# Keys and values in fixed lines: the order of a loop over eight groups of rows is written out, the value copy moves to VectorE, and a square root is written to PSUM

## The chip, the cores and the metric

The kernel runs on one core of a Trainium2 chip. The metric is device time in microseconds (us) of one execution; the time quoted for a kernel is the median of several executions.

## The reference, cut to what matters

The network has four parts on a residual stream x of 8 x 512 = 4096 rows of 128 floats, all in fp32: a local convolution, a small feed-forward network whose operands are quantised to four bits, a linear-attention part that trains a small network on its own keys and values, and a mixture of experts. Only the start of the third part is touched by this change:

```python
x = layernorm(x)
qkv = x @ qkv_w + qkv_b
q, k, v = jnp.split(qkv, 3, axis=-1)                    # 128 columns each
k = k.reshape(B, S, 16, 8)                              # 16 heads of 8
k = k / (jnp.linalg.norm(k, axis=-1, keepdims=True) + 1e-6) * kn_scale + kn_bias
...
for _ in range(2):                                      # training steps
    grads = jax.grad(loss_fn)(theta)                    # of mean((swish(k @ gate) * (k @ val)) @ proj - v)^2
    theta = muon_update(theta, grads)
```

The keys k and the values v of all 4096 rows must be there before the first training step has gone through them; the queries are made later, in pieces, between the steps.

## The kernel before, in words

The 4096 rows lie in SBUF as 32 tiles of 128 rows. They are worked on in `NG` = 8 groups of `G` = 4 tiles (512 rows). The stream x stays in SBUF for the whole kernel.

The kernel is written in a framework that takes the instructions of all engines in program order, works out the waits between them, and lets its own scheduler choose the order on each engine from due times it estimates. Where the author wants a fixed order he passes the instructions of an engine through a `Line` (line 105 of the kernel): each instruction of a line is put behind the one before it.

The touched stage is the first block of `ttt` (lines 824 to 863). For each group g it does this, in the order of its lines:

- `normal(g)`, lines 839 to 849. The layer norm's statistics come from VectorE, for four groups at once (`norm.stats`, `norm.newton`). ScalarE then applies them (`norm.apply`, line 583: four instructions of 128x128, tile `xn`), TensorE transposes `xn` (line 848, four matmuls against the identity), and ScalarE copies the transposed rows out of PSUM into `xt` (line 849).
- `rows_of`, line 799. TensorE multiplies the transposed rows by the key and value columns of the weight (four matmuls 128x256; the profile shows each as two records). The PSUM tile `rows` holds 4 x 256 numbers for each partition, two banks, and there are two such tiles.
- Line 856. ScalarE copies the value half into `v`.
- `heads`, lines 802 to 814. ScalarE squares the key half (line 805, tile `sq`); VectorE sums the squares of each head (line 807, 128x512 to 128x64, tile `nrm`); ScalarE takes the root in place (line 808); VectorE adds 1e-6 (line 809), inverts (line 810) and multiplies the keys by it (line 811, tile `k`).
- `turned`, lines 816 to 821. TensorE transposes the normed keys (line 820), and ScalarE takes them out of PSUM with the scale and shift of the heads (line 821, tile `kt`).
- Line 861. GpSimd applies the same scale and shift to the untransposed keys in place, two instructions. It may start only when the transposes of these keys have been read.

After the loop, line 863 adds a bias to each group of x on GpSimd; the scheduler spreads these eight instructions over the stage. The scheduler has put the normed rows `xn` of groups 0 to 3 ahead of the first `rows` matmul. From there its order on TensorE is: rows 0, rows 1, key transposes 0, `xn` transposes 2, rows 2, key transposes 1, `xn` transposes 3, rows 3, and so on: rows run one group ahead of the key transposes, and the transposes that rows are made from stand directly in front of them.

In front of the stage stands the last group of the feed-forward network (`fp4_ffn`, lines 627 to 730), whose quantisation goes back and forth: GpSimd scales (line 619, tile `v`), ScalarE takes magnitudes into PSUM (line 621), VectorE rounds (lines 622 and 623), GpSimd scales back (line 624, tile `hq`), TensorE transposes (line 708), ScalarE copies (line 711), TensorE multiplies (lines 714 and 716) and ScalarE writes x (line 720). Behind the stage stands `gradients` (lines 1073 to 1144), where for each tile TensorE has two forward products (lines 1087 and 1089), and GpSimd four instructions that make the derivative `ds` (lines 1100 to 1103).

Of the kernel before, what the change touches and what calls it, by code (L numbers as in the profile page):

```python
# [7 lines left out]
F32 = mybir.dt.float32  # L8
I32 = mybir.dt.int32
U32 = mybir.dt.uint32  # L10
AF = mybir.ActivationFunctionType
# [106 lines left out]
def grp(t, g):  # L118
    return t[:, g * G : (g + 1) * G, :]
# [434 lines left out]
class Norm:  # L554
# [1 line left out]


    def __init__(self, cx, pool, name, plus=0.0):
        self.cx, self.pool, self.name, self.plus = cx, pool, name, plus
        self.mv = pool.tile([P, NT, 2], F32, tag=f"{name}mv", name="mv")  # L560
        self.rs = pool.tile([P, NT], F32, tag=f"{name}rs", name="rs")
        self.off = pool.tile([P, NT], F32, tag=f"{name}off", name="off")
# [17 lines left out]
    def apply(self, g, dst):  # L580
        for j in range(G):
            i = g * G + j
            self.cx.nc.scalar.activation(
                dst[:, j, :], self.cx.x[:, i, :], AF.Identity, bias=self.off[:, i : i + 1], scale=self.rs[:, i : i + 1]
            )


UP = 1024
# [184 lines left out]
def ttt(cx):  # L773
# [10 lines left out]
    with ExitStack() as st:  # L784
# [6 lines left out]
        v = kv.tile([P, NT, D], F32, tag="v", name="v")  # L791
        kt = kv.tile([P, T], F32, tag="kt", name="kt")

        def rows_of(ps, tag, g, lo, hi):

            out = ps.tile([P, G, hi - lo], F32, tag=tag, name="rows")
            for j in range(G):
                at = slice(g * W + j * P, g * W + (j + 1) * P)
                nc.tensor.matmul(out[:, j, :], xt[:, at], w_qkv[:, lo:hi], start=True, stop=True)  # L799
            return out  # L800

        def heads(pool, src, dst):

            sq = pool.tile([P, G, D], F32, tag="sq", name="sq")
            nc.scalar.activation(sq, src, AF.Square)
            nrm = pool.tile([P, G, H], F32, tag="nrm", name="nrm")
            nc.vector.tensor_reduce(nrm, sq.rearrange("p j (h d) -> p j h d", d=DH), AX.X, ALU.add)
            nc.scalar.activation(nrm, nrm, AF.Sqrt)
            nc.vector.tensor_scalar(nrm, nrm, 1e-6, None, ALU.add)
            nc.vector.reciprocal(nrm, nrm)  # L810
            nc.vector.tensor_tensor(
                dst.rearrange("p j (h d) -> p j h d", d=DH), src.rearrange("p j (h d) -> p j h d", d=DH),
                nrm.unsqueeze(3).to_broadcast([P, G, H, DH]), ALU.mult,
            )

        def turned(ps, tag, src, i, dst):

            tp = ps.tile([P, W], F32, tag=tag, name="tp")
            for j in range(G):
                nc.tensor.transpose(tp[:, j * P : (j + 1) * P], src[:, j, :], cx.ident)  # L820
            nc.scalar.activation(dst, tp, AF.Identity, bias=cols[:, i, 1:2], scale=cols[:, i, 0:1])


        with ExitStack() as s1:
            wp = s1.enter_context(tc.tile_pool(name="c1_w", bufs=1))
            p2 = s1.enter_context(tc.tile_pool(name="c1_p2", bufs=2))
            ps = s1.enter_context(tc.tile_pool(name="c1_ps", bufs=4, space=PSUM))
            ps_q = s1.enter_context(tc.tile_pool(name="c1_psq", bufs=2, space=PSUM))
            norm = Norm(cx, wp, "ln", plus=1.0)
            total = ps.tile([P, 3 * D], F32, tag="t", name="total")  # L830
# [5 lines left out]
                nc.tensor.transpose(pp[:, c * P : (c + 1) * P], proj[:, c, :], cx.ident)  # L836
            nc.scalar.copy(proj_t, pp)

            def normal(g):
                if g % 4 == 0:  # L840
                    for i in range(g, g + 4):
                        norm.stats(i)
                    norm.newton(g, g + 4)
                xn = p2.tile([P, G, D], F32, tag="xn", name="xn")
                norm.apply(g, xn)
                tp = ps.tile([P, W], F32, tag="t", name="tp")
                for j in range(G):
                    nc.tensor.transpose(tp[:, j * P : (j + 1) * P], xn[:, j, :], cx.ident)
                nc.scalar.copy(xt[:, g * W : (g + 1) * W], tp)

            normal(0)
            for g in range(NG):
                if g + 1 < NG:
                    normal(g + 1)
                kvr = rows_of(ps_q, "kv", g, D, 3 * D)
                nc.scalar.copy(grp(v, g), kvr[:, :, D:])
                heads(p2, kvr[:, :, :D], grp(k, g))
                turned(ps, "t", grp(k, g), 1, kt[:, g * W : (g + 1) * W])
                r = grp(k, g).rearrange("p j (h d) -> p j h d", d=DH)
                for c, op in ((scale, ALU.mult), (shift, ALU.add)):  # L860
                    nc.gpsimd.tensor_tensor(r, r, c.unsqueeze(1).unsqueeze(1).to_broadcast([P, G, H, DH]), op)
            for g in range(NG):
                nc.gpsimd.tensor_tensor(grp(cx.x, g), grp(cx.x, g), b_o.unsqueeze(1).to_broadcast([P, G, D]), ALU.add)

        def queries(step):

            with ExitStack() as s3:
                pool = s3.enter_context(tc.tile_pool(name=f"q_p{step}", bufs=2))
                ps = s3.enter_context(tc.tile_pool(name=f"q_ps{step}", bufs=1, space=PSUM))
                for g in range(step * NG // STEPS, (step + 1) * NG // STEPS):  # L870
                    pq = rows_of(ps, "q", g, 0, D)
                    q = pool.tile([P, G, D], F32, tag="q", name="q")
                    heads(pool, pq, q)
                    yield
                    turned(ps, "q", q, 0, qt[:, g * W : (g + 1) * W])
                    yield


# [640 lines left out]
```

## Time and profile before

| what | value |
|---|---|
| median of three runs | 1273.8 us (1272.79 to 1276.15) |
| the profiled execution's own time | 1273.81 us |
| its span, first to last instruction | 1272.1 us |
| mean granted TensorE clock | 0.957 of full speed |
| busy share of the span: TensorE, VectorE, GpSimd, ScalarE | 86%, 60%, 58%, 39% |
| the touched stage, first `rows` matmul to the last group's key transposes | 400.14 to 441.17 us |

In the profile PE is TensorE, PEld its weight loads, DVE is VectorE, ACT is ScalarE and POOL is GpSimd. Times within an execution count from the start of the span. A row of the timeline has the start, the duration, the engine, the line and the tile written, and in brackets how long the engine was idle before and what released it. The granted clock (PEclk) is the share of full speed at which TensorE was let run.

### The profile page before, as it was taken

How to read it: one execution, taken by the hardware profiler on the slowest of the kernel's cores; microseconds unless marked ns; L12 is line 12 of the kernel's file. 1: busy time of each engine (PE TensorE's matmuls, PEld its weight loads, DVE VectorE, ACT ScalarE, POOL GpSimd, SP SyncE). 2: the span in 40 equal slices, each digit the busy share in tenths (PEclk: the TensorE clock that was granted, in tenths of full speed). 3: DMA queues.
4: the chain of work that ended last, by engine and by line, in shares of the span. 5: the costliest groups of instructions: out<-in, count | busy, mean ns of one | idle time of the engine just before them, and what ended most of it. 6: DMA issues, size and time to landing. Idle time of an engine off the chain costs nothing.

```text
span 1272.1 us, 15373 instructions
## 1 busy us (share of the span) xinstructions
PE 1090.9 (86%) x5219; PEld 650.0 (51%) x5219; DVE 765.5 (60%) x1761; ACT 494.0 (39%) x1009; POOL 743.3 (58%) x724
## 2 busy tenths in 40 slices
PE   5899998537877599999998899999989996599992
PEld 2334343225556445555557455555566664377872
DVE  6899999788885454444446444444455877033254
ACT  4646644346556632222234322222253342234331
POOL 3346755735554688888860688888700456355453
PEclk9899999958999999999999999999999998699997
DMA  5322444970000000000000000000000111212277
GB/s 152 87 79 80 124 110 139 356 208 1 1 1 1 0 1 1 1 1 1 1 1 1 0 1 1 1 1 1 1 1 1 34 39 46 62 51 68 68 183 212
DMA packets 66895, 67.26 MB, mean 53 GB/s; under 512 B 6928, under 2 KB 48735, under 8 KB 66817
## 3 DMA queue, kind: packets, MB, share of 16 engines
q1 hardware_dynamic: 59296, 56.57, 15.1%
q0 software_dynamic: 4608, 8.43, 2.1%
q10 hardware_dynamic: 2912, 1.29, 0.4%
q8 instruction: 41, 0.67, 0.2%
q14 instruction: 38, 0.30, 0.1%
HBM read 40.00 MB, written 27.13 MB: 53 GB/s over the span
## 4 chain that ended last, share of the span: by engine, by line
PE 50%; DVE 12%; ACT 5%; POOL 5%; issue 5%; DMA 2%; POOLq 0%; DVEq 0%; SPq 0%; ACTq 0%
PE ph L1135 5%; PE sum L1110 4%; PE pp L1125 4%; PE sum L1109 4%; PE sum L1111 4%; PE pa L1087 4%; PE ph L1429 4%; PE pb L1089 4%; PE po L1442 4%; PE pt L1118 2%; PE gu L692 2%; POOL v L619 1%; DVE ht L915 1%; PE a L975 1%; PE rows L799 1%
## 5 line engine op out<-in xcount | busy, mean ns | idle before, releaser
L1100 POOL TENSOR_TENSOR ds<-sw,s 128x512 f32<-128x512 f32 x64 | 81.7, 1276 | 86.8 <-DVE sw L1095 86.8
L1102 POOL TENSOR_TENSOR ds<-ds,s 128x512 f32<-128x512 f32 x64 | 111.4, 1740 | 5.0
L1330 POOL DMA_INDIRECT rows<-xr,slot x64 | 62.8, 982 | 73.8 <-DVE rs L93 45.1
L1093 ACT COPY b<-pb 128x512 f32<-128x512 f32 x64 | 37.5, 586 | 161.5 <-PE pb L1089 161.0
L1456 POOL DMA_INDIRECT res<-ye,xe x60 | 58.5, 975 | 66.2 <-DVE ye L1454 28.1
L1097 DVE TENSOR_TENSOR h<-sw,b 128x512 f32<-128x512 f32 x64 | 50.4, 787 | 70.6 <-ACT b L1093 70.3
L1432 ACT ACTIVATE ht<-ph,b 128x512 f32<-128x512 f32 (+2 forms) x100 | 55.9, 589 | 92.7 <-PE ph L1429 91.2
L402 POOL TENSOR_TENSOR pr<-base,en 128x512 f32<-128x512 f32 x48 | 72.7, 1545 | 32.4 <-ACT en L364 32.3
L1101 POOL TENSOR_TENSOR ds<-sw,ds 128x512 f32<-128x512 f32 x64 | 82.8, 1294 | 5.0
L1103 POOL TENSOR_TENSOR ds<-ds,b 128x512 f32<-128x512 f32 x64 | 81.5, 1273 | 5.0
L1125 PEld LDWEIGHTS pp<-proj,ht 128*128 128x128 f32 x512 | 67.1, 191 | 30.7 <-issue 29.4
L411 DVE TENSOR_TENSOR pr<-base,w 128x3072 f32<-128x3072 f32 x24 | 79.7, 3319 | 1.7 <-ACT w L362 1.7
L1120 ACT COPY ht<-pt 128x512 f32<-128x512 f32 x64 | 37.5, 586 | 102.1 <-PE pt L1118 102.1
L1442 PE MATMUL po<-w,ht 128*128 128x128 f32 (+1 forms) x640 | 77.1, 277 | 0.0
L1095 DVE TENSOR_TENSOR sw<-pa,s 128x512 f32<-128x512 f32 x64 | 44.2, 691 | 54.2 <-ACT s L1091 54.2
L1429 PE MATMUL ph<-xt,w 128*128 128x512 f32 (+2 forms) x200 | 72.8, 508 | 3.7 <-DVE xt L1417 3.7
L1442 PEld LDWEIGHTS po<-w,ht 128*128 128x128 f32 (+1 forms) x640 | 73.7, 187 | 0.7
L1137 DVE TENSOR_TENSOR db<-ph,sw 128x512 f32<-128x512 f32 x64 | 44.2, 691 | 47.1 <-PE ph L1135 47.1
L1135 PE MATMUL ph<-proj_t,dpt 128*128 128x512 f32 x128 | 71.6, 641 | 0.0
L420 PE MATMUL cv<-pr,sel 128*32 128x512 f32 x512 | 61.8, 612 | 9.7 <-DVE pr L411 9.2
L1087 PE MATMUL pa<-gate,kt 128*128 128x512 f32 x128 | 66.8, 604 | 2.5 <-ACT b L1093 2.4
L1110 PE MATMUL sum<-db,k 128*128 128x512 f32 x128 | 66.2, 598 | 1.6 <-DVE db L1137 1.6
(324 smaller groups left out, 2566.3 us busy)
## 6 DMA issues: line engine op xcount, KB each, us to landing
base<-far SPq DMA_DIRECT2D x64, 268.0 KB, 5.5
rows<-empty SPq DMA_DIRECT2D x1, 5005.0 KB, 16.9
res<-zero SPq DMA_DIRECT2D x1, 4096.0 KB
own<-zero SPq DMA_DIRECT2D x2, 2048.0 KB, 29.3
w<-in_L_ffn_W SPq DMA_DIRECT2D x16, 256.0 KB, 4.9
y<-res SPq DMA_DIRECT2D x16, 256.0 KB, 5.6
xe<-rows SPq DMA_DIRECT2D x7, 585.0 KB, 4.3
y<-own SPq DMA_DIRECT2D x12, 256.0 KB, 5.1
```

Source lines behind the costliest of these rows:

```text
L402: gp(nc.gpsimd.tensor_tensor(pr[:, d, :], s["base"][:, d, at], s["en"][:, g, :], ALU.mult))
L411: vec(nc.vector.tensor_tensor(s["pr"][g][:, :nv, :], s["base"][:, :nv, at], w.to_broadcast([P, nv, L]), ALU.mult))
L1087: nc.tensor.matmul(pa, ki, gate, start=True, stop=True)
L1100: nc.gpsimd.tensor_tensor(ds, sw, s, ALU.mult)
L1101: nc.gpsimd.tensor_tensor(ds, sw, ds, ALU.subtract)
L1102: nc.gpsimd.tensor_tensor(ds, ds, s, ALU.add)
L1103: nc.gpsimd.tensor_tensor(ds, ds, b, ALU.mult)
L1110: nc.tensor.matmul(sums[1], ki, db, **kw)
L1125: nc.tensor.matmul(pp, ht[:, c * P : (c + 1) * P], proj[:, c, :], start=(c == 0), stop=(c == NF - 1))
L1135: nc.tensor.matmul(ph, dpt, proj_t, start=True, stop=True)
L1429: ten(nc.tensor.matmul(ph[:, :n], self.w1[:, e, c * P : (c + 1) * P], xt[:, :n], start=True, stop=True))
L1442: ten(nc.tensor.matmul(po[:m, i - lo, :], ht[:, c, (i - lo) * P : (i - lo) * P + m], self.w2[:, e, c, :], start=(c == 0), stop=(c == NF - ...
```

## The change

The stage's loop is written again. Three `Line`s fix the order of its instructions on VectorE, TensorE and ScalarE.

- TensorE: `xn` transposes of group g+2, rows of group g+1, key transposes of group g. So rows are one group ahead of the key transposes, as before, and the `xn` transposes are now one group ahead of the rows made from them.
- The value copy goes from ScalarE (line 856 before) to VectorE (line 888 after).
- `heads` is split in two helpers. The root is written into a PSUM tile of its own (`root`, pool `ps_n`, one bank), and the addition of 1e-6 reads it from there. The pool `ps` has three banks in place of four.
- ScalarE's line: square of group g, take-out of the transposed keys of group g-1, root of group g, copy of the transposed rows of group g+2, application of the norm to group g+3.
- The statistics of groups 4 to 7 are asked for in the loop's second pass; the normed rows of groups 0 to 2 are prepared ahead of the loop and those of group 3 within it, with three buffers for `xn` in place of two.

The queries, which use `heads` and the transposing helper too, keep their instructions: their root stays in SBUF. The sums of squares, products and copies are the same numbers as before.

```diff
-        def heads(pool, src, dst):
+        def squares(pool, src, act=free, vec=free):
             sq = pool.tile([P, G, D], F32, tag="sq", name="sq")
-            nc.scalar.activation(sq, src, AF.Square)
+            act(nc.scalar.activation(sq, src, AF.Square))
             nrm = pool.tile([P, G, H], F32, tag="nrm", name="nrm")
-            nc.vector.tensor_reduce(nrm, sq.rearrange("p j (h d) -> p j h d", d=DH), AX.X, ALU.add)
-            nc.scalar.activation(nrm, nrm, AF.Sqrt)
-            nc.vector.tensor_scalar(nrm, nrm, 1e-6, None, ALU.add)
-            nc.vector.reciprocal(nrm, nrm)
-            nc.vector.tensor_tensor(dst..., src..., nrm..., ALU.mult)
+            vec(nc.vector.tensor_reduce(nrm, sq.rearrange("p j (h d) -> p j h d", d=DH), AX.X, ALU.add))
+            return nrm
+
+        def over_norm(src, root, nrm, dst, vec=free):
+            vec(nc.vector.tensor_scalar(nrm, root, 1e-6, None, ALU.add))
+            vec(nc.vector.reciprocal(nrm, nrm))
+            vec(nc.vector.tensor_tensor(dst..., src..., nrm..., ALU.mult))
...
-            ps = s1.enter_context(tc.tile_pool(name="c1_ps", bufs=4, space=PSUM))
+            ps = s1.enter_context(tc.tile_pool(name="c1_ps", bufs=3, space=PSUM))
+            ps_n = s1.enter_context(tc.tile_pool(name="c1_psn", bufs=1, space=PSUM))
...
-            normal(0)
+            roots(0)
+            for g in range(AHEAD):                      # AHEAD = 2
+                normal(g)
+                turns[g] = turn(ps, "t", normed[g])
+                keep_turn(g)
+            normal(AHEAD)
+            rows = rows_of(ps_q, "kv", 0, D, 3 * D, ten)
             for g in range(NG):
-                if g + 1 < NG:
-                    normal(g + 1)
-                kvr = rows_of(ps_q, "kv", g, D, 3 * D)
-                nc.scalar.copy(grp(v, g), kvr[:, :, D:])
-                heads(p2, kvr[:, :, :D], grp(k, g))
-                turned(ps, "t", grp(k, g), 1, kt[:, g * W : (g + 1) * W])
+                cur = rows
+                if g == 1:
+                    roots(FIRST)                        # statistics of groups 4 to 7
+                nrm = squares(p2, cur[:, :, :D], act, vec)
+                if g + AHEAD < NG:
+                    turns[g + AHEAD] = turn(ps, "t", normed[g + AHEAD], ten)
+                if g + 1 < NG:
+                    rows = rows_of(ps_q, "kv", g + 1, D, 3 * D, ten)
+                vec(nc.vector.tensor_copy(grp(v, g), cur[:, :, D:]))
+                if g:
+                    act(adjusted(kt[:, (g - 1) * W : g * W], tk, 1))
+                root = ps_n.tile([P, G, H], F32, tag="n", name="root")
+                act(nc.scalar.activation(root, nrm, AF.Sqrt))
+                if g + AHEAD < NG:
+                    keep_turn(g + AHEAD, act)
+                over_norm(cur[:, :, :D], root, nrm, grp(k, g), vec)
+                if g + AHEAD + 1 < NG:
+                    normal(g + AHEAD + 1)
+                tk = turn(ps, "t", grp(k, g), ten)
                 r = grp(k, g).rearrange("p j (h d) -> p j h d", d=DH)
                 for c, op in ((scale, ALU.mult), (shift, ALU.add)):
                     nc.gpsimd.tensor_tensor(r, r, c..., op)
+            act(adjusted(kt[:, (NG - 1) * W :], tk, 1))
```

## The prediction, made before the changed kernel was run

> **What bounds the kernel now.** I read the page's busy shares and slices first, then busy time by stretches, then the chain of waits through the touched stage, then the rows of single lines.
>
> ```profile
> PE 1090.9 (86%) x5219; PEld 650.0 (51%) x5219; DVE 765.5 (60%) x1761; ACT 494.0 (39%) x1009; POOL 743.3 (58%) x724
> PE   5899998537877599999998899999989996599992
> PEclk9899999958999999999999999999999998699997
> ```
>
> TensorE bounds most of the kernel, but its row of slices dips to 5 in slice 13, between a dense front and the dense gradients, and the granted clock dips there too. That is the touched stage. Busy time in it, and in two short stretches:
>
> ```profile
> 399.50:442.10 42.60, 25.29 (x121) 19.33 (x122) 23.78 (x55) 26.50 (x57) 22.80 (x18) 0.93 0.00 0
> ...
> 408.00:412.00 4.00, 3.42 (x8) 2.75 (x9) 2.50 (x3) 2.21 (x7) 3.11 (x3) 0.58 0.00 0
> ...
> 440.00:444.00 4.00, 2.83 (x7) 1.80 (x8) 1.01 (x2) 0.78 (x1) 2.58 (x3) 0.50 0.00 0
> ```
>
> Columns are stretch, length, PE, PEld, DVE, ACT, POOL, clock, DMA. No engine is busy for more than 26.5 of 42.6 us: the stage is bound by latency, by one engine waiting for another. The chain of waits shows the circle; here are two of its turns:
>
> ```profile
> 422.33 0.67 PE tp L820 x4
> 423.02 0.78 ACT kt L821
> 423.80 0.48 ACT xt L849
> 424.27 0.50 ACT sq L805
> 424.77 1.14 ACT xn L583 x3
> 425.91 0.15 ACT nrm L808
> 426.09 0.20 DVE nrm L809
> 426.32 0.56 DVE nrm L810
> ...
> 426.98 0.70 DVE k L811
> ...
> 427.72 0.67 PE tp L820 x4
> 428.42 0.78 ACT kt L821
> 429.19 0.48 ACT xt L849
> 429.67 0.16 ACT nrm L808
> 429.86 1.27 DVE nrm L809
> 431.16 0.56 DVE nrm L810
> ...
> 431.81 0.70 DVE k L811
> ...
> 432.56 0.67 PE tp L820 x4
> ```
>
> One turn is 5.39 us, the next 4.84. Every group's key transposes wait for work that stands on ScalarE behind the previous group's transposes. In the first turn the square and three norm instructions (1.6 us) stand ahead of the root; in the second the addition of 1e-6 takes 1.27 us where it took 0.20. That row on its own:
>
> ```profile
> L809 DVE TENSOR_SCALAR nrm<-nrm x16: 182/195/1265, 404.9 to 955.7; 128x64 f32<-128x64 f32 x16
> ```
>
> Minimum, median, maximum in ns. In the timeline the long ones end with a GpSimd instruction on the keys (one from 408.66 to 409.92, the addition until 409.97): VectorE is held while GpSimd runs. In the stage it happens to groups 1, 3 and 5 for 1.07 us each and to group 7 for 0.2.
>
> **The change part by part.** The orders of both kernels on each engine agree line for line before the last group of the feed-forward network and again from the first gradient matmul; SP's queue is the same, no DMA moves. So the sum is over two places, the stage and the tail in front of it.
>
> *Stage, one turn in the steady part.* Durations are from the timeline; t is from a group's square. The square takes 0.60, sum of squares 0.69 and so the root can start at 1.35. Between them ScalarE takes out the keys of the group before (0.67 from its start to the next), then root 0.15, copy of xt 0.46, four norm instructions 1.53 (0.383 each): the next square issues at 3.5. VectorE: sum at 0.65, value copy behind it (0.68, the row of the PSUM copies of line 988), addition at 1.88, inverse 2.11, product 2.78 to 3.47. TensorE: key transposes 3.52 to 4.18. Their take-out on ScalarE may start at 4.2, that is 0.7 into the next turn, and is over at 1.37, just when the root is due: no wait is added, but there is no slack. TensorE then has 0.5 for the xn transposes and 2.0 for the rows, done at 6.6, while the square that needs them is at 7.0. The turn is 3.5 us, set by ScalarE and the sum between square and root. The value copy costs VectorE 8 x 0.68 = 5.5 us, hidden in the wait for the root (its product ends at 3.47, the next sum starts at 4.15). Were that cover gone, 0.6 us a turn.
>
> *Stage, whole.* From the first rows matmul (R = 0; 400.14 before): square 0 at 2.0, table load 1.28, root 0 at 3.95, xt copy, norm of group 3, square 1 at 6.1. VectorE still has the rest of the statistics of groups 4 to 7 in front of the addition of group 0, so its product ends at 6.7, key transposes to 7.4 (before: 7.1). Take-out of group 0 to 8.1, root 1, xt, norm 4, square 2 at 10.3. Squares 3, 4, 5 at 13.8, 17.3, 20.85. Then no norm is left: square 6 at 23.95 and 7 at 27.0, now limited by TensorE (0.5 + 2.0 + 0.5). The last key transposes follow at 27.0 + 0.6 + 0.7 + take-out of group 6 0.67 + root, addition, inverse, product 1.9 = 31.0. Before it was 441.17 - 400.14 = 41.03. **Gain 10.0 us.** Of it 3.4 is the addition no longer held by GpSimd; the rest is the square, norm and xt copy leaving the circle.
>
> *The root in PSUM against a rule.* The Trainium skill, "VectorE: DVE Perf Modes", section "The perf-mode tier table", says that an fp32 scalar operation runs at double rate from SBUF and at single rate with any PSUM operand; with its table of cycles (58 + n/2 against 120 + n, at 0.96 GHz) I estimate 94 against 192 ns. It speaks against the change: 8 x 0.1 = 0.8 us lost. The trace has no such row with 64 columns; the nearest, copies of 128x128 from PSUM in line 1028, take 0.291 us, those of 128x512 in line 988 take 0.685, which is 1.03 ns a column, so 64 columns are 0.225. Against the measured 0.195 this is 0.03 a group, 0.2 in all; I take that, as both ends are rows of this trace. Bounds: 0 to 0.8 lost, against 3.4 won if PSUM operands are not held. The product (one PSUM operand) is 691 to 692 ns in all eight groups, whatever GpSimd did; so I expect no hold.
>
> *Tail of the feed-forward network.* On ScalarE two of the norm instructions of group 2 now stand among the last groups' work, and on TensorE two transposes of `hq` stand ahead of all eight `gu` matmuls of the last group. On GpSimd one bias addition (1.27) stands ahead of that `hq`. Before:
>
> ```profile
> 377.88 2.07 PEld L692 LDWEIGHTS gu<-w_in,xt 128*128 128x128 f32 x8 [0.96 <-ACT xt L684]
> ...
> 378.21 1.39 POOL L624 TENSOR_TENSOR hq<-v,sc 128x704 f32<-128x704 f32 x1 [1.47 <-DVE v L623]
> ```
>
> Followed through: GpSimd's second scaling ends at 376.6, bias addition 377.9, `hq` 379.4, so `gu` starts at 379.8 in place of 377.9. Half comes back where TensorE had waited for VectorE at 381.2; the inverse scale of the first half is then behind two `ht` copies on ScalarE, GpSimd's scaling starts at 386.7 for 383.7, and the last `hq` ends at 394.8 for 393.3. From there all is as before. **Cost 1.4 us**; bounds 0 (before's waits absorb it) and 3.0 (the whole delay of the scaling).
>
> *Clock.* At 408.6 the clock fell to half for 3.4 us, after TensorE had been idle for 2.7 us, busy 1.1 and idle 0.9: rows took 3.68 for 1.99. The skill's "TensorE: Matmul & The Clock Gate", Part 1, asks for an idle gap over 3.4 us. Here no gap was that long and the clock fell twice (second time after 1.13 and 2.83 us of idleness around 0.66 of work). By the rule neither kernel would lose it; by the trace the new order, idle 2.3 us after rows 1, may lose 1.7 us again. An even chance: **0.7 us lost**. By the rule alone I would forecast 0.7 less. At the gradients' start the gaps before and after are alike (2.6 for 2.8), counted as equal.
>
> *GpSimd and the hand-over.* It has 21 instructions from the bias of group 3 (6.5 after R) on: 21 x 1.34 = 28.2, done at 34.7, 3.7 after the last key transposes start. Before it was free 3.8 after (444.97), and the first `ds` came at 446.76, so 1.8 us were to spare. It becomes busy all through but is not late; from 1.9 us more it would delay the first `ds`, and behind that the third tile's sigmoid, which waited 1.4 us for a `ds` instruction to let go of its buffer.
>
> *Sum.* 1273.81 - 10.0 + 0.2 + 1.4 + 0.7 = 1266.1, from the profiled execution (1.7 us lie outside its span), which equals the median of 1273.80. I forecast **1266 us**. A measurement of this kernel can tell 0.3%, 3.8 us, from no change.
>
> **The rivals.**
>
> *GpSimd is the bound.* Its instructions take 1.6 us in the gradients beside VectorE's products of two SBUF tensors. If they did so here, 21 x 1.67 = 35.1, 6.9 later; less 1.9 to spare, some 5 us of the gain go: 1271. Against it: all 16 key instructions took 1.261 to 1.271 though VectorE worked beside them. Chance 0.06.
>
> *PSUM does not free the addition* (the change does not do what it says). GpSimd now runs without a gap, so each addition would be held, by about 0.7 on average, and the circle has no slack: 8 x 0.7 = 5.6 plus 1 of knock-on: 1272.5. Against it stand the unheld product and the PSUM copies (678 to 692). Chance 0.07.
>
> *TensorE's clock stays at half in the loop: slower.* Then a group is 2 x 1.12 of transposes and 3.68 of rows, 5.9 us where ScalarE needs 3.5: 8 x 5.9 = 47 for 41, plus 1.4: 1281. It decides when the busy share of some 3.4 us falls to the 0.32 to 0.38 that preceded the two falls; above one half none was seen (1.7 of 3.4 us at 415.4). The new loop has 3.1 of 3.5, so it should hold. Chance 0.04.
>
> *The fixed lines hold less well* (the take-out of keys comes a little late, the root waits, the turn is 4 us): 3 us less gain, 1269. Chance 0.13; the forecast has 0.70.
>
> **How the numbers follow.** The forecast's own range is 1262 (no tail cost, no half clock, and the second fall of the clock gone too) to 1269. The 0.13 case reaches 1270, GpSimd's 1271. With 1261 to 1271 I leave out about 0.15. Faster by over 0.3% (below 1270.0): the forecast and most of the 0.13 and some of the rest, 0.83. Within 0.3%: 0.11. Slower: the half clock and what I have not seen, 0.06.
>
> **What the changed profile would show.** Key transposes 3.5 us apart in the middle groups and about 31 from the first rows to the last; ScalarE without gaps there; the addition at 0.2 to 0.25 in every group; value copies of 0.68 on VectorE with no one waiting; `gu` of the last feed-forward group after `hq`; GpSimd unbroken for 28 us, the first `ds` not later against the first gradient matmul than 4.7 us. I am wrong if the turn is over 4 us, if the addition still shows 1.2, or if the tail costs over 3 us.

## The result, and the profile after

| kernel | median of its executions | kernel before beside it | ratio, 95% interval |
|---|---|---|---|
| changed kernel, 13 executions | 1268.91 us (1266.87 to 1271.15) | 1273.79 us | 0.9967 (0.996 to 0.9974) |
| the same on another chip, 13 | 1270.19 us (1268.09 to 1272.57) | 1273.31 us | 0.9979 (0.997 to 0.9988) |

On these two chips the changed kernel is faster by 3 to 5 us. The forecast was 1266.0, with 1261 to 1271 as its range. On a third chip the kernel before took 1304.78 us, and the four profiles taken there (all of the new loop) show the mixture of experts, which begins at about 975 us, some 28 us longer than the profiles from the other chips; the changed kernel took 1299.41 us there, a ratio of 0.9959 (0.9942 to 0.9975). From that chip only ratios and the stretches before 975 us are used.

The first profile of the changed kernel has a span of 1267.8 us (1272.1 before). Its page, busy time and slices:

```profile
PE 1093.3 (86%) x5219; PEld 653.2 (52%) x5219; DVE 770.7 (61%) x1769; ACT 489.5 (39%) x1001; POOL 742.0 (59%) x724
PE   5899997547877799999999899999989996599992
PEclk9899999958989899999999999999999997699996
```

VectorE has 5.2 us more and ScalarE 4.5 less: the eight value copies. The dip in slice 13 is shallower (7 for 5), and the clock line has more dips beside it. Busy time in the stage, in three of its turns and at the start of the gradients (columns as before: stretch, length, PE, PEld, DVE, ACT, POOL, clock, DMA):

```profile
402.10:435.40 33.30, 23.60 (x121) 19.50 (x122) 25.18 (x63) 24.13 (x53) 23.87 (x19) 0.91 0.00 0
413.60:424.30 10.70, 8.25 (x49) 6.67 (x48) 7.98 (x15) 10.43 (x25) 10.36 (x9) 1.00 0.00 0
408.50:412.50 4.00, 3.30 (x12) 3.03 (x13) 3.08 (x6) 3.19 (x9) 3.24 (x3) 0.57 0.00 0
432.90:443.20 10.30, 8.12 (x13) 3.38 (x14) 4.38 (x5) 3.73 (x5) 7.07 (x7) 0.50 0.01 2
```

In the middle turns ScalarE and GpSimd are now busy for 10.4 of 10.7 us, where no engine had been busy for more than 26.5 of 42.6. The first rows matmul starts at 402.79 and the last key transposes at 434.30: 31.51 us for 41.03. The last two rows are the clock at half. One turn in the chain of waits:

```profile
413.67 0.61 ACT sq L808
414.28 0.02 issue
414.30 0.70 DVE nrm L810
415.00 0.02 issue
415.02 0.23 ACT root L892
415.25 0.52 ACT xt L870
415.77 0.46 ACT xn L583 x2
416.23 0.21 issue
416.44 0.87 ACT xn L583 x2
417.31 0.49 ACT sq L808
```

From square to square it is ScalarE and one VectorE sum, with the key transposes outside the circle. By the timeline the squares start 3.54 us apart here, and 3.52 in each of the next two turns. The addition and the value copy, by their lines:

```profile
L815 DVE TENSOR_SCALAR nrm<-root x8: 214/216/225, 407.6 to 432.6; 128x64 f32<-128x64 f32 x8
L888 DVE COPY v<-rows x8: 680/680/682, 406.1 to 431.4; 128x512 f32<-128x512 f32 x8
```

No addition is held, though GpSimd works beside them with hardly a gap (10.36 of 10.70 us in the middle turns). What was not foreseen in its size is the tail of the feed-forward network, from VectorE's and ScalarE's timeline:

```profile
386.93 1.09 DVE L614 TENSOR_SCALAR sc<-sc 128x44 f32<-128x44 f32 x1
...
388.81 0.89 DVE L622 SCALAR_TENSOR_TENSOR v<-up,v 128x704 f32<-128x704 f32 x1
389.61 1.26 DVE L849 SCALAR_TENSOR_TENSOR w_qkv<-L_attn_qkv_b,w_qkv 128x384 f32<-128x384 f32 x1
390.80 0.88 DVE L623 SCALAR_TENSOR_TENSOR v<-up,v 128x704 f32<-128x704 f32 x1
...
391.77 0.76 ACT L621 ACTIVATE up<-v 128x704 f32<-128x704 f32 x1 [2.84 <-DVE v L623]
```

The correction of the key/value weight (L849) stands between the two steps of the rounding. The next `up` waits 2.84 us, because there is one `up` buffer and the second step (L623) lets go of it.

*Where the 4.3 us of span went, engine times set against those of the kernel before.* Up to the last group of the feed-forward network the two kernels are alike, and the changed one is 1.1 ahead: 2.7 from its start, less 1.6 in two longer half-clock stretches at 293 and 320 us. Of the rest, 3.76 is lost from there to the first rows matmul (0.9 of it by a half-clock stretch of 6.8 us at 365 where the kernel before has 3.4), 9.52 won in the stage, 0.8 lost at the start of the gradients (10.2 us at half clock for 6.8), 1.5 lost in the second training step, some 0.3 lost after it.

### The profile page after: what moved, and what is told of

Read it like the earlier page. It is cut to its first block, busy times and chain, and to the rows that moved or that the text cites. A ratio compares the mean times of both kernels' runs of the same rounds, so it can differ in the third digit from the quotient of the medians.

```text
span 1267.8 us, 15384 instructions
## 1 busy us (share of the span) xinstructions
PE 1093.3 (86%) x5219; PEld 653.2 (52%) x5219; DVE 770.7 (61%) x1769; ACT 489.5 (39%) x1001; POOL 742.0 (59%) x724
## 4 chain that ended last, share of the span: by engine, by line
PE 52%; DVE 13%; ACT 4%; issue 4%; POOL 4%; DMA 3%; POOLq 0%; SPq 0%; DVEq 0%; ACTq 0%
PE ph L1176 5%; PE sum L1151 4%; PE pp L1166 4%; PE sum L1150 4%; PE pa L1128 4%; PE po L1483 4%; PE pb L1130 4%; PE ph L1470 4%; PE sum L1152 4%; PE pt L1159 2%; PE gu L692 2%; DVE ht L956 1%; POOL v L619 1%; DMA y<-own 1%; PE a L1016 1%
## 5 line engine op out<-in xcount | busy, mean ns | idle before, releaser
L1166 PE MATMUL pp<-proj,ht 128*128 128x128 f32 x512 | 67.6, 275 | 0.0
```

Source lines behind the costliest of these rows:

```text
L1166: nc.tensor.matmul(pp, ht[:, c * P : (c + 1) * P], proj[:, c, :], start=(c == 0), stop=(c == NF - 1))
```

## The experiments

Stage and tail in all profiles. "Tail" is from the last `xt` copy of the feed-forward network (L684) to the first rows matmul, "stage" from there to the last key transposes, "turn" the distance of the middle squares; in the two kernels with the old order, where squares come in pairs, it is the distance of the key transposes.

| kernel | tail | stage | turn | half clock in the tail / in the loop, us |
|---|---|---|---|---|
| before | 22.90 | 41.03 | 5.39, 4.84 | 0 / 3.4 |
| changed | 24.84 | 31.51 | 3.52 | 0 / 3.4 |
| changed, second profile | 24.82 | 30.55 | 3.51 | 0 / 0 |
| changed, third | 26.76 | 31.63 | 3.52 | 6.8 / 3.4 |
| root in SBUF | 24.83 | 32.74 | 3.80 to 3.95 | 0 / 0 |
| value copy on ScalarE | 24.84 | 31.97 | 3.79 | 0 / 0 |
| both (order alone) | 26.64 | 33.69 | 3.78 to 3.93 | 6.8 / 3.4 |
| before + root in PSUM | 22.89 | 40.24 | 5.3 to 5.5, one 3.83 | 0 / 6.8 |
| bias late | 24.10 | 31.63 | 3.51 | 0 / 3.4 |
| weight correction last | 23.78 | 31.64 | 3.52 | 0 / 3.4 |
| two ScalarE instructions more | 26.79 | 31.63 | 3.52 | 6.8 / 3.4 |
| candidate, both profiles | 23.06 | 31.63, 31.64 | 3.52 | 0 / 3.4 |
| candidate, `hq` behind `gu` | 23.14 | 31.64 | 3.52 | 0 / 3.4 |

Rows are to be compared at equal half clock. One stretch in the loop costs about 1.0 (31.51 to 31.64 for 30.55), the one in the tail 1.9 (26.76 for 24.82).

**Root back in SBUF.**

```diff
-                root = ps_n.tile([P, G, H], F32, tag="n", name="root")
+                root = p2.tile([P, G, H], F32, tag="root", name="root")
```

> The changed kernel with one tile moved: the root is written to SBUF again (pool p2), nothing else; the order on every engine is that of the changed kernel. Theory (the PSUM root frees the addition from GpSimd, which now runs without a gap): the addition is held in most groups, by between 0 and 1.07 us, 0.5 on average, and since the turn of 3.52 us has no slack between root and product, the stage grows by 3 to 6 us: 1272 to 1275, about 1.003 of the changed kernel. Rival 1 (the lines alone did it, the hold falls into a wait): the addition is held, but the stage grows by 1 us or less: 1269 to 1270. Rival 2 (the hold came from the order, and no longer occurs): the addition takes 0.19 to 0.2 in all eight groups, time 1268.7.

Measured: 1271.51 us, 0.9987 (0.9978 to 0.9995) of the kernel before. The addition's line:

```profile
L815 DVE TENSOR_SCALAR nrm<-root x8: 186/720/870, 406.2 to 432.2; 128x64 f32<-128x64 f32 x8
```

It is held in seven of eight groups, by 0.2 to 0.7. The stage is 32.74 against 30.55, 2.2 us more. The hold is real, and a PSUM operand avoids it; but the price is below the expected 3 to 6, as the seven holds sum to 3.4 us over the free 0.19 and part of that falls into waits. The Trainium skill, "SBUF — State Buffer", section "SBUF: two separate sides", says that VectorE, in a mode that uses two ports, and GpSimd take a shared pair of SBUF ports for a whole instruction, while the one that comes second stands still; 0.186 to 0.870 from SBUF against 0.214 to 0.225 from PSUM, beside the same GpSimd instructions, agrees with it.

**Value copy back on ScalarE.**

```diff
-                vec(nc.vector.tensor_copy(grp(v, g), cur[:, :, D:]))
+                act(nc.scalar.copy(grp(v, g), cur[:, :, D:]))
```

> The changed kernel with the value copy back on ScalarE, in ScalarE's line between the square and the take-out of the keys; all else is as in the changed kernel. Theory (ScalarE is full in the turn of 3.52 us and sets it): ScalarE's turn grows by the copy, 0.48 us, in the groups that have a norm to apply (five), and by up to 0.48 in the three others: turn 4.0 us, stage 31.5 + 2.4 to 3.9, time 1271.3 to 1272.8. Rival (the turn is set by the chain through TensorE and VectorE, ScalarE has room): turn 3.5 to 3.6, time within 1 us of the changed kernel, 1269 to 1270.

Measured: 1270.34 us, 0.9981 (0.9972 to 0.999). ScalarE's turn in its timeline:

```profile
416.33 0.60 ACT L808 ACTIVATE sq<-rows 128x512 f32<-128x512 f32 x1
416.81 0.60 ACT L888 COPY v<-rows 128x512 f32<-128x512 f32 x1
417.27 0.81 ACT L836 ACTIVATE kt<-tp,cols 128x512 f32<-128x512 f32 x1
417.95 0.25 ACT L892 ACTIVATE root<-nrm 128x64 f32<-128x64 f32 x1
418.09 0.62 ACT L870 COPY xt<-tp 128x512 f32<-128x512 f32 x1
418.57 1.68 ACT L583 ACTIVATE xn<-x,off,rs 128x128 f32<-128x128 f32 x4
420.12 0.61 ACT L808 ACTIVATE sq<-rows 128x512 f32<-128x512 f32 x1
```

ScalarE now waits for nothing, and the turn is 3.79: 0.27 more, not 0.48, since 0.21 of the turn of 3.52 was idle. The stage is 1.4 longer than the 30.55 without half clock. The theory holds, with less than its price. The times alone do not tell this kernel from the changed one (0.9967 and 0.9979); the profile does.

**Both undone: the order alone.** The two edits above together.

> The changed kernel with two of its parts undone at once: the root in SBUF and the value copy on ScalarE; what is left is the new order (the three lines, the xn transposes one group ahead of the rows). Measured so far, by the profiles: with the root alone in SBUF the turn was 3.85 us and the stage 32.7, with the copy alone on ScalarE 3.79 and 32.0, with both as changed 3.52 and 30.6 to 31.6; the root alone, added to the kernel before, took 0.8 off 41.0. Theory (the order carries nearly all of the gain; hold and copy add up, since both stand between one root and the next): turn 4.0 to 4.3 us, stage 33.5 to 35, time 2 to 3.5 us above the changed kernel beside it. Rival 1 (the hold and the copy hide each other: VectorE is held while ScalarE copies): turn 3.8 to 3.9, stage 32.5 to 33. Rival 2 (the order without the two parts falls back into alternation as before): turn over 4.6, stage over 37.

Measured: 1271.55 us, 0.9987 (0.998 to 0.9993); the changed kernel beside it 1270.19. Stage 33.69 with one stretch of half clock, so some 32.7 without: the same as with the root alone in SBUF. Rival 1 is right for the turn of 3.8: hold and copy hide each other. At equal half clock the order alone takes 41.03 to 33.69, 7.3 of the 9.5 us. Moving the copy brings nothing while the addition is held, the PSUM root brings 0.7 while ScalarE is full (32.7 to 31.97), and both together 2.1. These figures rest on one profile each, and where a profile has half clock in the loop, on 1.0 us taken off for it.

**Root in PSUM alone, in the kernel before.**

```diff
-            nc.scalar.activation(nrm, nrm, AF.Sqrt)
-            nc.vector.tensor_scalar(nrm, nrm, 1e-6, None, ALU.add)
+            root = nrm if rp is None else rp.tile([P, G, H], F32, tag="n", name="root")
+            nc.scalar.activation(root, nrm, AF.Sqrt)
+            nc.vector.tensor_scalar(nrm, root, 1e-6, None, ALU.add)
```

> The kernel before with one part of the change alone: the root goes into a PSUM tile of its own (pool ps three banks in place of four); the order on every engine is that of the kernel before. Theory (a PSUM operand frees the addition, and this part is worth a third of the gain by itself): the addition takes 0.22 in all eight groups, three holds of 1.07 and one of 0.2 go, 8 x 0.03 come: stage 41.0 - 3.2 = 37.8, time 1270.6, ratio 0.9975. Rival (the hold was no cost of its own: what stands behind it, the next root or ScalarE's order, is late anyway): stage 40 to 41, time 1273 to 1274, ratio 0.9995.

Measured: 1273.21 us, 1.0001 (0.9992 to 1.001). All eight additions take 0.22 to 0.23, and the time does not move: of the expected 3.2 the profile shows 0.8 in the stage. The interval leaves room for 1 us either way: it excludes the 3.2, not the 0.8. The rival's figures (stage 40 to 41, time 1273 to 1274) came out. TensorE's timelines show where the holds went:

```profile
409.59 2.67 PE L799 MATMUL rows<-w_qkv,xt 128*128 128x256 f32 x6
412.09 0.60 PE L820 MATMUL tp<-ident,k 128*128 128x128 f32 x4
...
414.09 1.99 PE L799 MATMUL rows<-w_qkv,xt 128*128 128x256 f32 x8 [0.96 <-ACT xt L849]
...
419.14 3.49 PE L799 MATMUL rows<-w_qkv,xt 128*128 128x256 f32 x8 [0.91 <-ACT xt L851]
422.47 0.60 PE L821 MATMUL tp<-ident,k 128*128 128x128 f32 x4
...
427.86 0.66 PE L821 MATMUL tp<-ident,k 128*128 128x128 f32 x4 [1.40 <-DVE k L812]
...
431.69 0.60 PE L821 MATMUL tp<-ident,k 128*128 128x128 f32 x4
```

The first three of these lines are of the kernel before, the others of this one. The turn from 427.86 is 3.83 us where before it was 4.84: there the theory's 1.0 is won, in group 5. Group 3's turn, up to the transposes at 422.47, fell into a second half-clock stretch that the kernel before does not have: its rows took 3.49 for 1.99, and the key transposes start right behind them, with no wait for VectorE. There the turn is 5.33 us for 4.84, and the freed addition was no longer what came last. Group 1's hold had cost nothing even in the kernel before: its addition was held until 409.97, but the rows beside it ran at half clock (the last six of their eight records took 2.67, where eight take 1.99 at full clock), and the key transposes at 412.09 start right behind them. So of the three holds of 1.07 us, one was worth its full length here. That the clock takes group 3's gain in every execution is not shown by one profile.

**Bias additions behind the first step's gradients.**

```diff
             for g in range(NG):
-                nc.gpsimd.tensor_tensor(grp(cx.x, g), grp(cx.x, g), b_o..., ALU.add)
...
-                gradients(cx, s2, step, k, v, kt, gate, val, proj, proj_t, grads)
+                made = gradients(cx, s2, step, k, v, kt, gate, val, proj, proj_t, grads)
+                for g in range(NG if step == 0 else 0):
+                    add = nc.gpsimd.tensor_tensor(grp(cx.x, g), grp(cx.x, g), b_o..., ALU.add)
+                    after(tc, add, made)
```

> The changed kernel with the eight bias additions on GpSimd moved from the feed-forward network's tail and the stage to behind the first step's gradients; the order on TensorE, VectorE and ScalarE is unchanged. Theory (the bias addition ahead of hq is half of the 2.65 us that the tail lost): hq comes 1.26 us earlier, gu follows 1.3 earlier, the first rows matmul comes 1 to 1.5 us earlier; the stage keeps its 31.5 us; GpSimd has gaps in the stage (16 instead of 22 instructions); time 1267.3 to 1268.0. If GpSimd bounded the hand-over to the gradients (my first rival in the prediction), the first ds would come earlier against the last key transposes too, by 2 us or more, and the time would be 1265 to 1266. If the tail's loss lies elsewhere (the weight correction on VectorE): within 0.4 us of the changed kernel. The eight additions, 10 us on GpSimd, now run beside the weight update; should VectorE be held by them there, up to 2 us are lost again.

Measured: 1270.55 us, 0.9982 (0.9975 to 0.9988): not better than the changed kernel. The tail is 0.74 shorter, less than expected, because `hq` then waits for VectorE's rounding. GpSimd's last key instruction still ends 3.8 us after the last key transposes start, and the first `ds` comes as late as before, so GpSimd was no bound at the hand-over, although it had fewer instructions to do. In the weight update 2.5 us are lost; one place of it, in the timelines of GpSimd and VectorE:

```profile
657.11 9.84 POOL L925 TENSOR_TENSOR x<-x,L_attn_proj_b 128x512 f32<-128x512 f32 x8 [4.09 <-ACT grad L1186]
...
662.26 1.07 DVE L815 TENSOR_SCALAR nrm<-nrm 128x64 f32<-128x64 f32 x1
...
665.96 1.02 DVE L995 TENSOR_SCALAR nrm<-nrm 128x3 f32<-128x3 f32 x1 [0.71 <-ACT nrm L994]
```

These two take 0.20 and 0.17 in the changed kernel: the same hold, 1.7 us together. A half-clock stretch at 665 follows, so not all of the 2.5 is accounted for one by one.

**Weight correction behind the last rounding.**

```diff
-            nc.vector.tensor_tensor(b_qkv, b_qkv, total, ALU.subtract)
+            after(tc, nc.vector.tensor_tensor(b_qkv, b_qkv, total, ALU.subtract), cx.rounded, sync=False)
```

Here `cx.rounded` is the instruction of line 623.

> The changed kernel with the two instructions that correct the key/value weight (L848 and L849) put on VectorE behind the last rounding of the feed-forward network; on TensorE four transposes of proj and two of xn change places with transposes of hq. Theory (in the tail L849, 1.26 us, stands in front of the rounding L623, whose end lets go of the only `up` buffer): L623 comes 1.2 us earlier, the next up, the last hq and the first rows matmul follow; from the last xt copy of the feed-forward network (L684) to the first rows matmul 23.6 us for 24.84; time 1.2 us below the changed kernel beside it. Rival (it is the bias addition alone that delays the tail; TensorE or GpSimd would be late anyway): 24.5 to 24.9 us, time within 0.4 us.

Measured: 1297.05 us; on that chip the changed kernel had 1299.41, with some 2 us of interval on each, so the price is read from the profile. Tail 23.78, 1.04 shorter. `up` now waits 1.78 for 2.84:

```profile
389.76 0.89 DVE L623 SCALAR_TENSOR_TENSOR v<-up,v 128x704 f32<-128x704 f32 x1
...
390.75 0.76 ACT L621 ACTIVATE up<-v 128x704 f32<-128x704 f32 x1 [1.78 <-DVE v L623]
```

**The changed kernel again, twice.**

> The changed kernel itself once more, as the yardstick for the runs beside it. Expected: 0.9967 of the kernel before (0.996 to 0.9974), the turn of 3.52 us and the stage of 31 to 32 us as in its first profile. What its second profile is to tell: whether the half-clock stretches (10.2 us at the start of the gradients, 3.4 at 320 us, none of them in the kernel before) belong to the change or to this execution. Theory (they vary from execution to execution): at least one of the two is gone or has another length. Rival (they belong to the order of the changed kernel): both are there again. The late b copies of ScalarE in the second step, at 801.7 and 911.0 us, which cost 0.85 and 0.68 us, are in all profiles of the new loop and should be there again.

> The changed kernel a third time, as the yardstick beside the other runs of this call: 0.9967 of the kernel before, stage 30.6 us without a half-clock stretch in the loop, 31.5 to 31.6 with one; the late b copies in the second step again (0.85 and 0.68).

The half-clock stretch at 320 us is gone in both; the one at the gradients' start is 10.2 us in the second profile and 3.4 in the third. The one in the loop is absent in the second, and the third has one of 6.8 in the tail, where neither the kernel before nor the first two show any (columns as above; third profile, then second):

```profile
392.50:400.50 8.00, 6.76 (x37) 5.98 (x36) 1.20 (x8) 1.99 (x4) 1.38 (x1) 0.57 0.00 0
...
392.50:400.50 8.00, 6.44 (x53) 5.79 (x53) 2.00 (x10) 2.24 (x4) 1.38 (x1) 1.00 0.00 0
```

So these stretches change from execution to execution (in the loop, nine of the twelve profiles with the new loop have one), and the changed kernel's times spread with such stretches. The late `b` copies are there in both.

**Two ScalarE instructions more.**

```diff
                 act(nc.scalar.activation(root, nrm, AF.Sqrt))
+                for _ in range(2 if g == NG - 1 else 0):
+                    act(nc.scalar.copy(spare, xt[:, :1]))
```

> The changed kernel with two more ScalarE instructions (copies of one column, in the last pass of the loop); the order on all engines stays, but ScalarE's instruction stream is two longer from there on, as it is in the kernel before. Theory (an instruction whose number in ScalarE's stream is 63 modulo 128 starts some 0.3 us late, and the new loop's shorter stream has put this number from the sigmoid s, where it hides, onto the copy b, where it makes VectorE's product collide with GpSimd): the late b copies at 801.7 and 911.0 us are gone, the sigmoid of the same tile is 0.3 us late in their place, and the second step is 1.5 us shorter (0.85 + 0.68); the time is 1 to 1.5 us below the changed kernel beside it. Rival 1 (the late copies have to do with the data or with the time): they stay, time within 0.4 us. Rival 2 (the collision only moves to other tiles): one or two others of 0.7 to 0.9 us appear, time within 0.4 us.

Measured: 1299.04 us against 1299.41, with intervals of some 2 us: the times settle nothing. The profiles do. First the changed kernel (third profile), then this one:

```profile
801.26 0.58 ACT L1134 COPY b<-pb 128x512 f32<-128x512 f32 x1 [3.15 <-PE pd L1172]
...
801.88 1.53 DVE L1138 TENSOR_TENSOR h<-sw,b 128x512 f32<-128x512 f32 x1 [1.51 <-ACT b L1134]
...
799.09 0.60 ACT L1135 ACTIVATE s<-pa 128x512 f32<-128x512 f32 x1 [0.55 <-DVE da L1183]
802.27 0.59 ACT L1137 COPY b<-pb 128x512 f32<-128x512 f32 x1 [2.59 <-PE pb L1133]
802.89 0.76 DVE L1141 TENSOR_TENSOR h<-sw,b 128x512 f32<-128x512 f32 x1 [1.23 <-ACT b L1137]
```

The late copy (idle 3.15 for the 2.87 or 2.59 of other tiles) is gone, the sigmoid is 0.28 late in its place (0.55 for 0.27), and the product `h` no longer falls onto a GpSimd instruction (0.76 for 1.53). From here on every time is 0.85 earlier than in the changed kernel, when both are set against the kernel before, and another 0.68 from the second place on, as expected. There is a second effect that I had not expected: the first `ds` comes 4.62 after the last key transposes, for 5.55. The next experiment has the same and shows where it comes from.

**A candidate: weight correction last, bias additions behind the last scaling, the two instructions.** To the two edits above it adds:

```diff
-                nc.gpsimd.tensor_tensor(grp(cx.x, g), grp(cx.x, g), b_o..., ALU.add)
+                add = nc.gpsimd.tensor_tensor(grp(cx.x, g), grp(cx.x, g), b_o..., ALU.add)
+                after(tc, add, cx.scaled, sync=False)
```

Here `cx.scaled` is the instruction of line 624.

> A candidate for a better version: the changed kernel, with the weight correction behind the last rounding (as in the run with that alone), all bias additions on GpSimd behind the last scaling hq of the feed-forward network (four of them then fill the time in which GpSimd waits for the first keys, four stay among the keys), and the two ScalarE instructions more. If the three act one by one: 0.75 (the bias alone gave that at the first rows matmul) + 1.2 + 1.5 = 3.4 us below the changed kernel, 1265 to 1266, ratio to before 0.994. If the weight correction and the bias addition hide each other: 2.3 us below. If the additions at the start of the stage hold VectorE's corrections and statistics: up to 1.3 of it comes back.

> The candidate of the last call once more (weight correction behind the last rounding, bias additions behind the last scaling, two ScalarE instructions more), beside the changed kernel on one chip. By its profile, what it took off the changed kernel was 1.76 us before the first rows matmul and 1.53 in the second step. Expected: 3.0 to 3.5 us below the changed kernel's median, ratio to before 0.994. If the clock's half-speed stretches eat it: 1.5 to 2.5 us.

Measured, first: 1296.24 us, 0.9934 (0.9914 to 0.9954), beside 1299.41 for the changed kernel. Second: **1263.19 us, 0.9923 (0.991 to 0.9936)**, beside 1270.19 and, for the kernel before, 1273.31. The tail is 23.06 in both, 1.76 shorter. The second run's 7 us are more than the 3.0 to 3.5 expected. By its profile against the third of the changed kernel: 1.8 of the tail, 1.9 of the half clock there, 0.9 at the hand-over, 1.5 in the second step, 6.1 together; the two spans differ by 5.0, and where the tail begins this execution of the candidate is 0.8 behind. The hand-over to the gradients, third profile first, then the candidate:

```profile
435.79 0.78 ACT L836 ACTIVATE kt<-tp,cols 128x512 f32<-128x512 f32 x1 [2.84 <-PE tp L831]
...
437.53 1.28 ACT L1132 ACT_TABLE_LOAD   x1 [0.96 <-PE pa L1128]
...
432.91 0.78 ACT L836 ACTIVATE kt<-tp,cols 128x512 f32<-128x512 f32 x1 [2.51 <-PE tp L831]
433.71 1.28 ACT L1136 ACT_TABLE_LOAD   x1
```

With the two copies, in this run as in the one with the copies alone, the load of the sigmoid's table no longer stands behind ScalarE's wait for the first forward product: 0.96 us of waiting turn into loading. Why two copies change which wait stands ahead of the load was not tried.

**And the transposes of `hq` behind all eight `gu` matmuls.** The edit puts them behind the fourth; in the trace they stand behind all eight.

```diff
-                    nc.tensor.transpose(
+                    tr = nc.tensor.transpose(
                         tp[: part[c], j * P : (j + 1) * P], hq[:, j, c * P : c * P + part[c]], cx.ident
                     )
+                    if g == NG - 2:
+                        after(tc, tr, gus[g + 1, 1], sync=False)
```

> The candidate with one thing more: on TensorE the transposes of the second-to-last group's hq stand behind all eight gu matmuls of the last group of the feed-forward network, where in the changed kernel two of them stand ahead. Theory (gu then waits for its transposed rows alone, as in the kernel before): gu 1.0 us earlier (0.64 after the xt copy for 0.64 to 1.5), its second half 0.6 earlier, the first rows matmul 22.5 us after L684 for 23.06; 0.6 us below the candidate. Rival (the second half of gu waits for VectorE's h in any case): 23.0, no difference over 0.2 us; or slower, if the transposes of hq, now behind gu, delay the output product and with it the x copy.

Measured: 1262.76 us, 0.9925 (0.9912 to 0.9938), and a tail of 23.14: no difference. `gu` starts 0.64 after the `xt` copy in both, so once the bias addition is out of the way `hq` is in time, and the theory falls.

## Why the prediction was right, point by point

*The turn, 3.5 us.* 3.52. That ScalarE sets it is nearly so: 0.21 of it was idle.

*The stage, 31.0 and a gain of 10.0.* 31.51 in the profile, 30.55 where no half clock fell into the loop; the gain is 9.5 with one stretch of half clock in both kernels. Not only the sum came out: the squares of the second profile stand 4.1, 3.8, 3.5, 3.5, 3.5, 2.9 and 3.1 us apart, for 4.1, 4.2, 3.5, 3.5, 3.55, 3.1 and 3.05 written.

*"Of it 3.4 is the addition no longer held."* Wrong as a share. The order brings 7.3 by itself, the other two parts 2.1, and only together; in the old order the freed addition moved the time by nothing that the runs can tell. Summing the holds priced a delay without asking what stood next behind it; behind group 1's stood rows at half clock.

*The root in PSUM: 0.03 a group, no hold.* Right: 0.216 for an estimate of 0.225. The table's 94 and 192 ns were both below what was measured (182 to 195 from SBUF, 214 to 225 from PSUM); the difference the trace gave was the better guide.

*Tail, 1.4 us.* This is the term that was mis-sized. From the `xt` copy of the group before to the first rows matmul, the second profile, which has no half-clock stretch that the kernel before lacks, needs 2.85 more than the kernel before. The first profile needs 3.76 more and the third 4.88, with more half clock. So one of the signs of being wrong, a tail that costs over 3 us, came true in two of three profiles. The working is right as far as the scaling on GpSimd: it starts at 385.71 in the second profile, which is 1.09 ahead, so at 386.8 for 386.7 written. But the last `hq` then ends 2.9 later than before, where only 1.5 was written: the working let half of the delay come back, and 0.2 came back. It missed that the weight correction moves ahead of L623, worth 1.04 by experiment, with the one `up` buffer behind it. The bias addition, which the working had, is worth 0.74 by experiment. And 0.93 of the 2.85 is lost ahead of the last `xt` copy, as far as the lines show; the second profile first, then the kernel before:

```profile
375.90 0.76 ACT L621 ACTIVATE up<-v 128x704 f32<-128x704 f32 x1 [1.40 <-DVE v L623]
...
378.13 0.76 ACT L621 ACTIVATE up<-v 128x704 f32<-128x704 f32 x1 [0.30 <-DVE v L623]
```

In the new order this second `up` stands in front of the `xt` copy on ScalarE (at 377.08) and waits 1.40 for the first half's rounding; before, it stood behind the copy (at 377.24).

*Clock, 0.7 us at even chances.* Right in kind, too large in size: where the clock fell in the loop it cost 1.0, not 1.7, and it fell in nine of twelve profiles. It never stayed at half there, as the third rival had it. Not foreseen was the stretch in the tail, 1.9 us, in three of the seven profiles that have the changed kernel's own tail. The rule that I used asks for a gap over 3.4 us, and the gaps were shorter. The page that it is from, "TensorE: Matmul & The Clock Gate", Part 1, also says that the window in which activity is counted runs freely, so that the same kernel meets it at another phase. That agrees with these profiles, and I had not used it. In the third profile TensorE was busy for 1.39 us of the 3.41 in front of the stretch at 393.0, and the clock fell; in the profile of the root in SBUF, whose stretches put the window at 389.97 to 393.38, the same place has 1.55, and it stayed. Moved over the tail, such a window finds TensorE busy for as little as 0.35 of it in the changed kernel, but nowhere for less than 0.54 in the candidate or with the weight correction last. By the limit worked out in the last section the candidate cannot fall into this stretch, and neither of its profiles shows it.

*GpSimd and the hand-over.* Right that it is not late: its last key instruction ends 3.77 us after the last key transposes start (3.7 written), and the first `ds` waits 1.78 for VectorE, as before. The agreement of the two figures is in part luck. The 3.7 was a backlog, but GpSimd stands idle for 1.13 us before its last two key instructions, until the last key transposes are done, and with the bias additions moved away it ends just as late.

*What the sum did not have:* 1.53 in the second training step, from a ScalarE stream of another length.

*The sum.* The median landed 2.9 above 1266.0. In the span of the first profile, -7.7 us was written (-10.0, 0.2, 1.4 and 0.7) and -4.3 measured. The stage with its clock gave 9.5 for 9.1. The tail took 3.76 for 1.4. The start of the gradients (0.8), the second step (1.5) and what follows it (0.3) had been put at nothing. The 1.1 by which this execution was ahead before the last group of the feed-forward network has nothing to do with the change and is luck; without it the sum would have been off by 4.5.

## What to carry to other kernels

In a loop bound by latency, write down the circle and see which instruction is waited for last; a single stall taken out of it may bring next to nothing, and two changes that each bring little can bring two microseconds together. When a scheduler reorders what stands in front of the touched loop, follow each moved instruction to the buffer that the one behind it lets go. Set a moved instruction against the whole stream of its engine, too: what runs beside it on GpSimd, and where it puts the clock's pauses, can outweigh its own time.

## What the runs showed of the hardware that was not expected

- Half-clock stretches are multiples of 3.41 us (3.4, 6.8, 10.2, 30.7, 34.1), but for a last one that the end cuts off. So the 14 profiles can be cut into windows of 3.41 us, counted on from the stretches of each. Between 300 and 1050 us the clock fell behind 56 windows, and in all of them TensorE was busy for 0.43 of the window or less (1.45 of 3.41 us before 418.8 with the root in PSUM alone); behind the 2926 windows at full clock with 0.45 or more it never fell. No single gap need be long: 2.21 us was the longest in front of the third profile's stretch in the tail. Before 300 and after 1050 us the two ranges overlap, so the limit is shown for this part of the kernel only.
- Where these windows lie differs between executions. Those whose first stretch begins at 36.9 to 37.0 us (three profiles: 10.2 us at 293 and 3.4 at 320) or at 39.9 to 40.2 (five: 6.8 at 296, none at 320) agree with each other up to the change. But of four that begin at 38.9 to 39.2, one (the order alone) has 10.2 us at 292 and 3.4 at 319 and the others do not. What the clock costs an execution is in part set by where its windows fall.
- ScalarE started the instructions numbered 575, 703, 959 and 1087 of its stream (counted from 0 with the waits; all are 63 modulo 128) 0.28 us later than their like. At number 191 nothing of the kind shows. In the kernel before number 959 is a sigmoid, which hides it; in the changed kernel 959 and 1087 are copies `b`, and each then makes VectorE's product collide with GpSimd. In the transfers of the trace an 8 KB instruction fetch goes out shortly after such places, at 802.6 us for the copy at 801.7. That the fetch is the cause is only argued; that the position matters is shown by the two added instructions.
- VectorE's hold by GpSimd reaches very small instructions: an addition of 128x3 took 1.02 us for 0.17.
